# Attention and graph layers on one Trainium2 core: four-row tables, one ring of row tiles, deviations by logarithm, new step times

## Chip, core and metric

The kernel runs on one core of one Trainium2 chip. TensorE (PE in the profile) multiplies matrices into PSUM, VectorE (DVE) and ScalarE (ACT) work elementwise and along rows, GpSimd (POOL) makes small products and issues indirect DMAs, SyncE (SP) issues most other DMAs. Each engine runs its own instructions in program order and waits on semaphores for the others. The metric is device time in microseconds, as the median of several runs; the profile is one execution beside them.

## What is computed

```python
# x: (32, 512, 1024), adj: (512, 512), wq, wk: (512,), bm: (512,), bias: (1024,)
h = relu(layernorm(x))                       # over the last axis
q = einsum('c,bcn->bn', wq, h);  k = einsum('c,bcn->bn', wk, h)
s = leaky_relu(q[:, None, :] + k[:, :, None], 0.01)
agg = einsum('bcn,bmn->bcm', h, softmax(s, -1))
x = x + relu(einsum('oc,bcm->bom', adj, agg) + bm[None, :, None])
h = relu(layernorm(x))
x = x + einsum('bnf,nm->bmf', h, adj * adj) + bias
```

Everything is float32. The scores matrix has rank one before the leaky slope, so the kernel never forms it. It sorts the 1024 columns of a batch by q: for a given k the terms with positive score are a suffix of the sorted list, the others a prefix, and the weighted sums of all suffixes and prefixes give every output row.

## The kernel before

A batch passes through a chain of steps. `load` brings four row tiles of 128 x 1024, `stats`, `norm`, `slopes` and `relu` normalise them (lines 409 to 436: variance, square root on ScalarE, reciprocal on VectorE, then one activation a tile). `scores` gives q and k, `row` broadcasts q to all partitions through DRAM, `columns` turns q and k. `rank` (VectorE) counts for each column how many q are smaller, `lower` (ScalarE) how many are below -k. `value` multiplies h by adj's transpose, eight tiles of 128 columns, and `spread` copies each out of PSUM. `to_rows` turns ranks into table rows, `scatter` writes each value row (512 values and its q, 513 in all) into one of five DRAM tables at its sorted place. `fetch` reads the sorted table back in nine blocks, `weights` makes exponentials of q, and nine `scan` steps multiply a masked, weighted matrix with a block; each step does a suffix block and a prefix block in the two halves of TensorE's columns. `sums` copies each step's last row into the next block (the carry) and writes all sums to the table. `gather` fetches for each output column one suffix sum, one prefix sum and the single value between them as 3 x 513 values in one row; `excess`, `divide`, `weigh` and `combine` mix them, `turn` transposes the result and adds it to rows of x that `reload` has brought again. The second layer follows: `stats`, `norm`, `slopes`, `relu` into new h tiles, `lift` (bias), `propagate` (512 x 512 squares of adj) and `finish`, which adds and writes out.

What sets the order: every step has a time in the table `PLAN` for each of its parts, plus 80.647 for each batch; `FIRST` and `LAST` shift and stretch the times of the first and last five batches. All steps of all batches are sorted by these times and issued in that order, each engine getting its instructions in it. The numbers are only an order: the real distance between batches is what the engines make of it. In the middle of the run steps of four or five batches alternate, for instance values of batch 15 with scans of 13 and 14, propagates of 11 and turns of 12.

Row tiles come from three pools: `xp` with 7, `yp` with 7 and `hp` with 4 buffers; x tiles are loaded into `xp` (the second batch's and three of the third's into `yp`), reloaded y tiles into `yp`, h of layer 1 into `hp`. A tile's buffer is free after its last reader. Table i of the five holds slots of three rows (suffix sum, prefix sum, even value), and a second half for the odd values; 126 values and two fixed rows make one block of 128. The two fixed rows come from `pads`, one step with 20 DMAs on SP. `fetch` needs two DMAs per three blocks, for even and odd rows.

Of the kernel before, what the change touches and what calls it, by code (L numbers as in the profile page):

```python
# [10 lines left out]
BF16 = mybir.dt.bfloat16  # L11
# [9 lines left out]
DATA = 126  # L21
PAIRS = 63
# [3 lines left out]
TABLES = 5  # L26
PLAN = {
    "adjacency": (-108.2,),
    "biases": (103.637,),
    "columns": (-0.644,),  # L30
    "combine": (
        295.175, 296.981, 297.681, 298.56, 293.456, 294.898, 296.312, 299.441, 298.758,
        299.991, 297.356, 298.478, 299.289, 299.451, 296.18, 297.782,
    ),
    "compare_mask": (-39.924,),
    "divide": (279.776,),
    "excess": (274.084,),
    "factors": (31.052,),
    "fetch": (71.51,),
    "finish": (356.071, 361.635, 372.571, 377.123, 391.802, 417.732, 398.837, 420.531),  # L40
    "from_rows": (87.236,),
    "gather": (260.35, 264.453, 263.071, 264.447, 267.501, 263.458, 263.983, 262.344),
    "later": (82.669,),
    "lift": (343.707, 352.288, 361.264, 350.629),
    "load0": (-132.547,),
    "load1": (-83.561,),
    "load2": (-110.642,),
    "load3": (-58.45,),
    "lower": (25.135, 20.956, 15.44, 19.087, 14.733, 13.756, 46.166, 37.237),
    "masks": (-18.987,),  # L50
    "norm0": (-31.509,),
    "norm1": (326.35,),
    "pads": (-73.925,),
    "propagate": (346.423, 349.207, 352.169, 365.765, 371.233, 382.761, 381.981, 389.706),
    "rank": (17.984, 18.872, 20.129, 19.992, 25.594, 25.16, 26.367, 26.318),
    "reload0": (283.236,),
    "reload1": (289.947,),
    "reload2": (275.592,),
    "reload3": (294.126,),
    "relu0": (-21.389, -21.25, -20.652, -20.617),  # L60
    "relu1": (336.308, 336.463, 336.836, 338.53),
    "row": (1.149,),
    "scan": (88.672, 94.082, 102.974, 119.344, 135.342, 151.67, 171.394, 183.726, 197.836),
    "scatter": (49.236, 49.927, 49.759, 49.383, 53.226, 50.436, 50.301, 52.611),
    "scores": (-2.312,),
    "slopes0": (-23.106,),
    "slopes1": (327.104,),
    "spread": (10.418, 15.798, 4.081, 13.981, 26.765, 25.953, 18.654, 18.733),
    "square": (58.25,),
    "stationary": (82.87, 113.617, 158.362),  # L70
    "stats0": (-66.042, -57.278, -62.987, -37.25),
    "stats1": (317.836, 318.803, 321.449, 320.562),
    "sums": (90.354, 96.928, 115.433, 127.043, 139.894, 157.148, 175.982, 190.223, 211.407),
    "to_rows": (21.507, 28.041),
    "totals": (87.7,),
    "turn0": (305.575, 305.673, 305.631, 305.894),
    "turn1": (311.888, 311.406, 311.889, 311.693),
    "turn_adjacency": (-56.308,),
    "value": (4.654, 14.383, -2.141, 4.319, 19.868, 19.769, 15.801, 17.456),
    "weigh": (288.834, 288.645, 287.955, 288.582, 291.515, 291.657, 292.795, 290.433),  # L80
    "weights": (79.137,),
}
FIRST = {
    "columns": ((-42.337, 0), (-5.231, 0), (-2.394, 0), (1.4, 0), (-0.267, 0)),
    "combine": (
        (1.654, -0.5293), (1.005, -0.3379), (12.151, -0.5389), (4.662, 1.8664), (-2.717, -0.8902),
    ),
    "divide": ((-6.522, 0), (2.121, 0), (-5.673, 0), (4.125, 0), (-1.132, 0)),
    "excess": ((-1.018, 0), (2.997, 0), (-2.579, 0), (2.459, 0), (2.332, 0)),
    "factors": ((12.008, 0), (36.085, 0), (20.556, 0), (-17.001, 0), (38.59, 0)),  # L90
    "fetch": ((-13.827, 0), (-9.161, 0), (-4.562, 0), (-10.853, 0), (-1.955, 0)),
    "finish": (
        (-7.71, -0.5057), (2.749, -0.1853), (2.024, 0.1345), (-9.528, -0.7581), (-1.467, 0.1212),
    ),
    "from_rows": ((-16.545, 0), (143.901, 0), (-18.52, 0), (2.567, 0), (44.362, 0)),
    "gather": (
        (-9.577, -0.9485), (-11.32, -0.6577), (-4.449, 0.1722), (-9.629, -0.1251), (0.796, 0.0714),
    ),
    "later": ((-7.518, 0), (-7.347, 0), (-5.042, 0), (-3.972, 0), (4.883, 0)),
    "lift": (  # L100
        (18.493, -0.0414), (7.449, -0.8273), (15.021, 1.1896), (12.507, -0.3341), (13.391, 1.5716),
    ),
    "load0": ((-55.083, 0), (-28.454, 0), (-82.787, 0), (-89.755, 0), (-8.172, 0)),
    "load1": ((-101.05, 0), (-75.105, 0), (-63.613, 0), (-51.655, 0), (-0.85, 0)),
    "load2": ((-75.638, 0), (-49.315, 0), (-74.213, 0), (-72.717, 0), (-4.898, 0)),
    "load3": ((-124.613, 0), (-99.018, 0), (-53.784, 0), (-32.124, 0), (2.903, 0)),
    "lower": (
        (-42.973, -0.9302), (-15.708, -0.6946), (-9.312, -0.2971), (10.582, -0.0696), (34.856, -0.2988),
    ),
    "norm0": ((-83.601, 0), (-72.105, 0), (-7.68, 0), (-14.053, 0), (-0.379, 0)),  # L110
    "norm1": ((7.168, 0), (3.555, 0), (4, 0), (0.017, 0), (-5.5, 0)),
    "propagate": (
        (2.872, -0.6898), (4.018, -0.2375), (-1.06, -0.345), (-1.214, -0.2813), (-1.309, -0.0657),
    ),
    "rank": (
        (-28.589, 0.7379), (-2.87, -0.0721), (-9.055, 1.3394), (2.403, 0.1874), (-13.459, 0.0458),
    ),
    "reload0": ((-6.546, 0), (6.572, 0), (3.271, 0), (5.826, 0), (-6.189, 0)),
    "reload1": ((-1.43, 0), (8.813, 0), (6.594, 0), (3.913, 0), (-1.301, 0)),
    "reload2": ((-12.374, 0), (4.019, 0), (-0.514, 0), (8.006, 0), (-11.757, 0)),  # L120
    "reload3": ((1.756, 0), (10.208, 0), (8.663, 0), (2.721, 0), (1.743, 0)),
    "relu0": (
        (-45.821, -0.4234), (-30.012, 0.2683), (5.354, 1.299), (-1.745, 0.0153), (3.565, -0.5324),
    ),
    "relu1": (
        (9.188, 0.8499), (2.193, -0.013), (10.49, -0.8921), (-4.148, -0.0533), (5.006, -0.1977),
    ),
    "row": ((-24.758, 0), (-11.86, 0), (-11.402, 0), (-3.047, 0), (-12.236, 0)),
    "scan": (
        (-10.549, -0.0092), (-6.067, 0.0274), (-9.758, -0.1074), (-3.442, 0.0619), (-0.102, -0.002),  # L130
    ),
    "scatter": (
        (-17.315, 0.2618), (-11.153, 0.1679), (0.523, -0.1955), (-0.018, 0.156), (10.696, 0.3981),
    ),
    "scores": ((-62.327, 0), (-16.533, 0), (-8.214, 0), (-8.615, 0), (-9.042, 0)),
    "slopes0": ((-60.963, 0), (-35.582, 0), (0.527, 0), (-21.398, 0), (0.491, 0)),
    "slopes1": ((7.724, 0), (5.221, 0), (19.376, 0), (1.394, 0), (7.329, 0)),
    "spread": (
        (-20.028, 0.1376), (-6.015, 0.992), (8.718, 0.232), (10.947, -0.0528), (-1.297, 0.1468),
    ),  # L140
    "stationary": (
        (-9.533, -0.0517), (-0.489, 0.0893), (-5.756, -0.1735), (-6.449, -0.1248), (4.497, -0.0251),
    ),
    "stats0": (
        (-104.674, 0.702), (-77.356, 0.023), (-31.203, 0.8527), (-27.97, 0.4148), (-4.885, 0.5116),
    ),
    "stats1": (
        (1.142, 1.1308), (0.139, -0.1099), (5.326, 1.0258), (1.699, -0.7252), (-0.894, -0.2163),
    ),
    "sums": (  # L150
        (-8.312, -0.031), (-5.309, 0.0498), (-7.225, -0.0992), (-0.666, 0.0426), (1.428, -0.0107),
    ),
    "to_rows": (
        (-22.19, 0.5865), (-4.005, -0.1384), (-1.537, -0.1666), (6.658, -0.9288), (6.396, -0.6681),
    ),
    "totals": ((-8.637, 0), (-5.524, 0), (-8.905, 0), (-5.244, 0), (1.382, 0)),
    "turn0": ((-0.966, 0.9178), (2.05, 1.1944), (5.507, -0.2416), (13.541, 1.3559), (6.422, 0.711)),
    "turn1": (
        (-5.235, 2.5311), (3.046, 0.3048), (6.19, 0.6659), (-2.074, -0.6081), (-2.371, 1.8837),
    ),  # L160
    "value": (
        (-38.477, -0.2052), (-18.574, 0.6364), (-1.298, 0.5607), (-3.097, 0.6813), (-5.339, -0.0078),
    ),
    "weigh": (
        (-11.307, 0.6182), (-3.966, -0.0933), (3.637, 0.3643), (2.741, 0.6417), (-2.168, 0.2103),
    ),
    "weights": ((-7.839, 0), (-5.68, 0), (-3.274, 0), (-1.31, 0), (1.823, 0)),
}
LAST = {
    "columns": ((7.408, 0), (2.218, 0), (11.624, 0), (6.617, 0), (9.298, 0)),  # L170
    "combine": (
        (184.23, -0.647), (7.018, -0.6426), (4.54, 0.7582), (4.732, 1.7176), (6.572, -0.8403),
    ),
    "divide": ((175.719, 0), (2.439, 0), (-3.673, 0), (2.742, 0), (4.328, 0)),
    "excess": ((172.709, 0), (3.234, 0), (1.536, 0), (-5.245, 0), (8.713, 0)),
    "factors": ((-5.036, 0), (-12.606, 0), (17.188, 0), (-12.641, 0), (7.562, 0)),
    "fetch": ((5.667, 0), (1.995, 0), (5.156, 0), (-1.217, 0), (1.341, 0)),
    "finish": (
        (752.974, -0.831), (173.796, 0.1634), (35.432, 0.5906), (9.597, -0.1536), (9.066, 0.2434),
    ),  # L180
# [616 lines left out]
```

## Time and profile before

| | us |
|---|---|
| median of 3 runs | 2378.45 (2374.22 to 2379.13) |
| profiled execution, span | 2372.9 |
| TensorE busy | 2295.2 |
| VectorE busy | 1952.6 |
| ScalarE busy | 1599.8 |
| GpSimd busy | 720.7 |
| 123 table loads on ScalarE | 158 |

The span runs from the first to the last instruction of the profiled execution; it lies 5.55 us below the median of the runs. In the profile L703 is the matmul of propagate (pg), L550 of value (pv), L639 and L636 of a scan (sc), L696 of turn (tr), L445 of scores (pq). A float32 matmul appears as two records. The DMA engines moved 643 MB, a mean of 271 GB/s; in the middle of the run they are busy about 0.9 of the time.

### The profile page before, as it was taken

How to read it: one execution, taken by the hardware profiler on the slowest of the kernel's cores; microseconds unless marked ns; L12 is line 12 of the kernel's file. 1: busy time of each engine (PE TensorE's matmuls, PEld its weight loads, DVE VectorE, ACT ScalarE, POOL GpSimd, SP SyncE). 2: the span in 40 equal slices, each digit the busy share in tenths (PEclk: the TensorE clock that was granted, in tenths of full speed). 3: DMA queues.
4: the chain of work that ended last, by engine and by line, in shares of the span. 5: the costliest groups of instructions: out<-in, count | busy, mean ns of one | idle time of the engine just before them, and what ended most of it. 6: DMA issues, size and time to landing. Idle time of an engine off the chain costs nothing.

```text
span 2372.9 us, 28069 instructions
## 1 busy us (share of the span) xinstructions
PE 2295.2 (97%) x7568; PEld 1011.5 (43%) x7568; DVE 1952.6 (82%) x5008; ACT 1599.8 (67%) x2880; POOL 720.7 (30%) x973
## 2 busy tenths in 40 slices
PE   7787999999999999999999999999999999999997
PEld 3233444444444444444444444444444444443443
DVE  7457888888888888888888888888888888888875
ACT  4576776766777766777676777676677676677551
POOL 2233333233333233233223233323333323233310
PEclk9988999999999999999999999999999999999998
DMA  6678888989999998999999999899988898998972
GB/s 222 171 181 277 284 284 277 296 269 276 287 290 285 296 286 266 277 299 283 288 292 266 276 294 287 287 291 272 268 291 276 288 302 253 276 282 269 311 294 79
DMA packets 206894, 643.45 MB, mean 271 GB/s; under 512 B 29120, under 2 KB 29248, under 8 KB 206736
## 3 DMA queue, kind: packets, MB, share of 16 engines
q1 hardware_dynamic: 142944, 355.74, 53.9%
q0 software_dynamic: 57344, 268.99, 30.7%
q10 hardware_dynamic: 6448, 16.92, 2.3%
q8 instruction: 61, 1.00, 0.2%
q14 instruction: 97, 0.79, 0.1%
HBM read 429.94 MB, written 211.60 MB: 270 GB/s over the span
## 4 chain that ended last, share of the span: by engine, by line
PE 85%; DMA 5%; DVE 5%; ACT 2%; issue 1%; POOL 1%; SPq 0%; ACTq 0%; another core or an unknown queue 0%; POOLq 0%; DVEq 0%
PE pg L703 34%; PE pv L550 33%; PE sc L639 10%; PE tr L696 4%; DMA vs<-td 2%; PE pq L445 2%; PE sc L636 1%; DVE g L689 1%; DVE st L414 1%; DMA g<-td,idg 1%; DMA td<-v,idx 1%; DVE junk L492 1%; ACT x L433 0%; DVE junk L487 0%; DMA x<-in_x_dram 0%
## 5 line engine op out<-in xcount | busy, mean ns | idle before, releaser
L703 PE MATMUL pg<-h,wsq 128*128 128x512 f32 x2048 | 911.2, 598 | 12.8 <-ACT h L433 12.8
L550 PE MATMUL pv<-wmT,x 128*128 128x512 f32 x2048 | 908.8, 598 | 5.9 <-ACT x L433 4.4
L703 PEld LDWEIGHTS pg<-h,wsq 128*128 128x128 f32 x2048 | 382.8, 191 | 517.4 <-issue 476.1
L550 PEld LDWEIGHTS pv<-wmT,x 128*128 128x128 f32 x2048 | 382.0, 191 | 499.1 <-issue 452.6
L623 POOL TENSOR_TENSOR sm<-mask_a,wc 128x192 f32<-128x192 f32 x96 | 51.9, 540 | 1254.9 <-DVE wc L600 785.7
L689 DVE SCALAR_TENSOR_TENSOR g<-g,cf 128x512 f32<-128x512 f32 x512 | 357.9, 756 | 46.4 <-ACT g L685 44.3
L648 ACT COPY vs<-sc 1x512 f32<-1x512 f32 x256 | 145.3, 567 | 272.9 <-PE sc L639 208.6
L563 POOL DMA_INDIRECT td<-v,idx x256 | 272.4, 1064 | 149.3 <-POOL v L562 36.3
L639 PE MATMUL sc<-vs,sm 128*64 128x512 f32 x1024 | 282.6, 621 | 21.3 <-POOL sm L623 11.1
L503 ACT ACTIVATE junk<-qrow,qk 128x1024 bf16<-128x1024 f32 x256 | 294.0, 1148 | 5.5 <-DMA qrow<-qd 2.5
L660 POOL DMA_INDIRECT g<-td,idg x256 | 243.5, 951 | 147.4 <-issue 71.5
L698 DVE SCALAR_TENSOR_TENSOR y<-tr,nbm,y 128x512 f32<-128x512 f32 x256 | 174.4, 744 | 66.3 <-PE tr L696 61.2
L711 DVE SCALAR_TENSOR_TENSOR y<-pg,bm_sb,y 128x512 f32<-128x512 f32 x256 | 185.8, 731 | 32.4 <-PE pg L703 32.0
L651 ACT COPY t<-sc 128x512 f32<-128x512 f32 x288 | 168.0, 583 | 40.7 <-DMA td<-t 35.3
L433 ACT ACTIVATE x<-x,nmr,rstd 128x1024 f32<-128x1024 f32 x128 | 148.6, 1231 | 64.9 <-DVE nmr L425 64.9
L492 DVE TENSOR_SCALAR_CACHE_REDUCE junk<-qrow,qk,cnt 128x896 bf16<-128x896 f32 (+6 forms) x224 | 180.5, 806 | 8.2
L685 ACT ACTIVATE g<-g,cf 128x512 f32<-128x512 f32 x256 | 167.7, 712 | 6.4 <-DVE cf L679 5.3
L487 DVE TENSOR_SCALAR_CACHE_REDUCE junk<-qrow,qk 128x128 bf16<-128x128 f32 (+6 forms) x224 | 166.0, 741 | 6.6
L414 DVE BATCH_NORM_STATS2 st<-x 128x6 f32<-128x512 f32 x256 | 162.7, 677 | 9.6 <-DMA x<-in_x_dram 9.6
L439 DVE TENSOR_TENSOR y<-y,bias_sb 128x1024 f32<-128x1024 f32 x128 | 154.3, 1219 | 16.0 <-ACT h L433 16.0
L557 ACT COPY v<-pv 128x512 f32<-128x512 f32 x256 | 141.8, 579 | 29.7 <-PE pv L550 14.0
L414 DVE BATCH_NORM_STATS2 st<-y 128x6 f32<-128x512 f32 x256 | 160.4, 668 | 0.0
(111 smaller groups left out, 1923.1 us busy)
## 6 DMA issues: line engine op xcount, KB each, us to landing
vs<-td SPq DMA_DIRECT2D x192, 384.8 KB
td<-t SPq DMA_DIRECT2D x576, 128.2 KB
x<-in_x_dram SPq DMA_DIRECT2D x128, 512.0 KB
y<-in_x_dram SPq DMA_DIRECT2D x128, 512.0 KB
out_dram<-y SPq DMA_DIRECT2D x128, 512.0 KB
qrow<-qd ACTq DMA_DIRECT2D x32, 512.0 KB
td<-v,idx POOLq DMA_INDIRECT x256, 8.3
g<-td,idg POOLq DMA_INDIRECT x256, 13.8
```

What stands on the lines that cost most here:

```text
L414: nc.vector.bn_stats(st[:, i, :], s.x[c][:, ts(i, HALF)])
L492: nc.vector.tensor_scalar(junk[:, j * P :], s.qrow[:, j * P :], qc, first, ALU.is_lt, ALU.add, accum_out=s.cnt[:, 1, j : j + 1],)
L503: nc.scalar.activation(junk, s.qrow, AF.Sign, bias=s.qk[:, 1, j : j + 1], accum_out=s.sgn[:, j : j + 1])
L550: nc.tensor.matmul(pv, s.h[c][:, ts(j, P)], wmT[:, c, :], start=(c == 0), stop=(c == NC - 1))
L563: i = nc.gpsimd.indirect_dma_start(tds[s.b % TABLES][:, :], bass.IndirectOffsetOnAxis(ap=s.idx[j // 4][:, j % 4 : j % 4 + 1], axis=0), v[: ...
L639: nc.tensor.matmul(p[ts(k, HP), :], m[:, k, :], s.vs[h][:, 0:C], start=True, stop=True)
L651: nc.scalar.copy(t[:, 0:C], p)
L660: nc.gpsimd.indirect_dma_start(s.g[:, j, :], None, tds[s.b % TABLES][0 : 3 * NB * HP, :].rearrange("(s k) w -> s (k w)", k=3), bass.Indire ...
L689: nc.vector.scalar_tensor_tensor(r, s.g[:, j, k * W : k * W + C], s.cf[:, k, j : j + 1], r, ALU.mult, ALU.add)
L698: nc.vector.scalar_tensor_tensor(xh, pt, nbm[:, o : o + 1], xh, ALU.max, ALU.add)
L703: nc.tensor.matmul(pg, wsq[:, r, ts(c, P)], s.h[r][:, ts(i, HALF)], start=(r == 0), stop=(r == NC - 1),)
L711: nc.vector.scalar_tensor_tensor(xh, s.pg.pop((c, i)), bm_sb[:, c : c + 1], xh, ALU.add, ALU.add)
```

## The change

- The table has four rows per pair of ranks: suffix sum, even value, prefix sum, odd value. A block holds 124 values (`RUN` is 31 pairs, twice per block) and two pairs of fixed rows; even and odd ranks alternate over the partitions, so one DMA fetches three blocks. The gather still reads three neighbouring rows, which start at the suffix row; even value and prefix sum change places in them. The index formulas get shorter for `to_rows`.
- `pads` becomes five steps, one per table, with two DMAs each.
- All row tiles (x, y, h) come from one pool of 18 (`ROWS`).
- The deviation's inverse is exp(-0.5 ln(var + eps)) on ScalarE, both functions from one table set that is loaded at the start, and three small operations on VectorE refine it by a Newton step.
- `rank` and `lower` write their unused elementwise output as uint8, not bfloat16; the two masks are made directly; q is kept in four DRAM rows by turns, not two.
- `PLAN`, `FIRST` and `LAST` have new numbers, the last two for six batches; the distance of 80.647 stays.

```diff
-    NB = N // DATA + 1
+    NB = N // (4 * RUN) + 1
-    xp = ctx.enter_context(tc.tile_pool(name="xp", bufs=7))
-    yp = ctx.enter_context(tc.tile_pool(name="yp", bufs=7))
-    hp = ctx.enter_context(tc.tile_pool(name="hp", bufs=NC))
+    xp = ctx.enter_context(tc.tile_pool(name="xp", bufs=ROWS))
...
     def sorted_rows(td, h, n):
-        rows = td.rearrange("(o h s k) w -> o s h k w", o=2, s=HP, k=3)
-        return rows[:, :, h : h + n, 2, :]
+        rows = td.rearrange("(h p k) w -> p h k w", p=P, k=2)
+        return rows[:, h : h + n, 1, :]
...
-    nc.scalar.activation(root, eps_sb, AF.Sqrt)
+    nc.scalar.preload_act_table_set("natural_log_exp_and_others")
...
-    def pads(s):
-        pad = vp.tile([P, W], F32, tag="v", name="pad")
+    def pads(s, i):
+        pad = vp.tile([P, W], F32, tag="v", name=f"pad_{i}")
         nc.vector.memset(pad, 0.0)
         nc.vector.memset(pad[:, C : C + 1], FAR)
-        for td in tds:
-            for o in range(2):
-                nc.sync.dma_start(sorted_rows(td, 0, NB - 1)[o, 0], pad[0 : NB - 1, :])
-                nc.sync.dma_start(sorted_rows(td, NB - 1, 1)[o, :, 0], pad[0:HP, :])
+        halves = tds[i].rearrange("(g o k) w -> g o k w", o=HP, k=2)[0 : 2 * (NB - 1), 0:2, 1, :]
+        nc.sync.dma_start(halves, pad[0 : 2 * (NB - 1), :].unsqueeze(1).broadcast_to([2 * (NB - 1), 2, W]))
+        nc.sync.dma_start(sorted_rows(tds[i], NB - 1, 1)[:, 0], pad)
...
     def masks(s):
+        for mask, k in ((mask_a, 1), (mask_b, -1)):
+            nc.vector.memset(mask, 1.0)
+            nc.gpsimd.affine_select(
+                out=mask, in_=mask, compare_op=ALU.is_gt, fill=0.0, base=0, pattern=[[-2 * k, HP]],
+                channel_multiplier=k,
+            )
...
     def norm(s, layer):
-        nc.scalar.activation(s.std, s.mv[:, :, 1], AF.Sqrt, bias=eps_sb)
+        nc.scalar.activation(s.std, s.mv[:, :, 1], AF.Ln, bias=eps_sb)
+        s.rstd = sp.tile([P, NC], F32, tag=f"rstd{layer}", name=f"rstd{layer}_{s.b}")
+        nc.scalar.activation(s.rstd, s.std, AF.Exp, scale=-0.5)
     def slopes(s, layer):
-        nc.vector.reciprocal(s.rstd, s.std)
+        nc.vector.scalar_tensor_tensor(t, s.mv[:, :, 1], EPS, s.rstd, ALU.add, ALU.mult)
+        nc.vector.scalar_tensor_tensor(t, t, -0.5, s.rstd, ALU.mult, ALU.mult)
+        nc.vector.scalar_tensor_tensor(s.rstd, t, 1.5, s.rstd, ALU.add, ALU.mult)
...
     def relu(s, layer, c):
-            pool, tag = (xp, "x") if s.b == B - 2 else (hp, "h")
-            h = pool.tile([P, N], F32, tag=tag, name=f"h_{s.b}_{c}")
+            h = xp.tile([P, N], F32, tag="x", name=f"h_{s.b}_{c}")
...
     def rank(s, j):
-        junk = wp.tile([P, N], BF16, tag="junk", name=f"junk_{s.b}_{j}")
+        junk = wp.tile([P, N], U8, tag="junk", name=f"junk_{s.b}_{j}")
...
+    def floor(rk, n, name, s):
+        f = sp.tile([P, rk.shape[1]], F32, tag=f"floor{name}", name=f"floor{name}_{s.b}")
+        nc.vector.tensor_scalar(f, rk, 1.0 / n, 0.5 / n - 0.5, ALU.mult, ALU.add)
+        nc.vector.tensor_scalar(f, f, ROUND, -ROUND, ALU.add, ALU.add)
+        return f
     def to_rows(s, i):
-        pair, block = pairs(rk, "q", s)
-        odd = 3.0 * NB * HP
-        nc.vector.tensor_scalar(rk, rk, odd, 5.0, ALU.mult, ALU.add)
-        nc.vector.scalar_tensor_tensor(rk, pair, 3.0 - 2.0 * odd, rk, ALU.mult, ALU.add)
+        f = floor(rk, 2 * RUN, "q", s)
+        nc.vector.tensor_scalar(rk, rk, 2.0, 5.0, ALU.mult, ALU.add)
-        nc.vector.scalar_tensor_tensor(s.idx[i], block, 3.0, rk, ALU.mult, ALU.add)
+        nc.vector.scalar_tensor_tensor(s.idx[i], f, 4.0, rk, ALU.mult, ALU.add)
     def from_rows(s):
-        pair, block = pairs(rk, "r", s)
+        pair = floor(rk, 2, "p", s)
+        f = floor(pair, RUN, "r", s)
-        nc.vector.scalar_tensor_tensor(s.idg, pair, 1.0, block, ALU.add, ALU.add)
+        nc.vector.tensor_tensor(f, f, pair, ALU.add)
+        nc.vector.tensor_scalar(s.idg, f, 4.0, 4.0, ALU.mult, ALU.add)
...
     def fetch(s):
-            for o in range(2):
-                d = nc.sync.dma_start(t[ts(o, HP)], sorted_rows(tds[s.b % TABLES], 3 * i, 3)[o])
+            d = nc.sync.dma_start(t, sorted_rows(tds[s.b % TABLES], 3 * i, 3))
...
     def sums(s, i):
-        td = tds[s.b % TABLES].rearrange("(s k) w -> s k w", k=3)
+        td = tds[s.b % TABLES].rearrange("(s k) w -> s k w", k=4)
         nc.sync.dma_start(td[ts(ha, HP), 0, :], t[0:HP, :])
-        nc.sync.dma_start(td[ts(hb, HP), 1, :], t[HP:P, :])
+        nc.sync.dma_start(td[ts(hb, HP), 2, :], t[HP:P, :])
```

Of the new times, those that the prediction speaks of, as they stand for the batches in the middle of the run:

```diff
-    "adjacency": (-108.2,),
+    "adjacency": (-988.26,),
-    "fetch": (71.51,),
+    "fetch": (33.445,),
-    "scan": (88.672, 94.082, 102.974, 119.344, 135.342, 151.67, 171.394, 183.726, 197.836),
+    "scan": (51.176, 57.633, 64.219, 81.673, 97.074, 108.292, 133.694, 146.062, 161.601),
-    "turn0": (305.575, 305.673, 305.631, 305.894),
+    "turn0": (264.575, 264.492, 264.401, 264.843),
-    "value": (4.654, 14.383, -2.141, 4.319, 19.868, 19.769, 15.801, 17.456),
+    "value": (-34.236, -39.683, -34.816, -23.667, -14.904, -27.47, -22.782, -17.741),
```

## The prediction

> **What bounds the kernel now.** I read the page first (busy shares and slices), then the chain that ended last, then TensorE's timeline at the head, in one steady batch and at the end.
>
> ```profile
> PE 2295.2 (97%) x7568; PEld 1011.5 (43%) x7568; DVE 1952.6 (82%) x5008; ACT 1599.8 (67%) x2880; POOL 720.7 (30%) x973
> ...
> PE   7787999999999999999999999999999999999997
> ...
> PEclk9988999999999999999999999999999999999998
> ```
>
> TensorE is busy 97% of the span; what it misses lies in the first four slices and the last. The chain puts a number on the middle:
>
> ```profile
> 440.35 3.63 PE pv L550 x8
> ...
> 510.88 3.63 PE pv L550 x8
> ```
>
> The same step of consecutive batches starts 70.53 us apart, and the stage between has TensorE 100% busy at full clock. 32 x 70.53 = 2257; the span is 2372.9. So 116 us are head and tail, and a change pays only there, or by shortening the 70.53. VectorE has about 61 us of work per batch, ScalarE 50: neither is the bound. In one batch (the chain again):
>
> ```profile
> 1086.36 3.28 PE sc L639 x12
> 1089.64 17.36 PE pv L550 x40
> 1107.00 1.87 PE sc L639 x8
> ...
> 1128.30 0.86 PE sc L636 x2
> ...
> 1142.95 1.01 PE sc L639 x4
> ```
>
> A scan step is 0.86 us in the full array (L636). In 64-column halves (L639, 4 records a step) one step takes 1.01 and two 1.87, so entering that mode costs 0.15; the 40 pv after it take 17.36 instead of 40 x 0.429 = 17.17, so leaving costs 0.19. Three steps should take 2.73 and take 3.28: 0.55 us is a stall, because two of them are consecutive steps of one batch and the second needs the row that ScalarE carries over.
>
> The head, TensorE's timeline (last bracket: idle before, and its releaser):
>
> ```profile
> 118.58 2.43 PE L639 MATMUL sc<-vs,sm 128*64 128x512 f32 x4 [4.39 <-POOL sm L623]
> ...
> 206.56 2.08 PE L636 MATMUL sc<-vs,sm 128*128 128x512 f32 x2 [8.93 <-ACT vs L649]
> ...
> 214.15 4.91 PE L696 MATMUL tr<-ident,g 128*128 128x128 f32 x32
> ...
> 263.34 17.43 PE L703 MATMUL pg<-h,wsq 128*128 128x512 f32 x40
> ```
>
> TensorE waits for scans whose rows were scattered and fetched late, then for the first gather.
>
> **What the Trainium skill says.** TensorEngine Tiling (Array Packing), Key Properties: changing the tiling mode drains TensorE; the 0.15 + 0.19 us above agree. TensorE: Matmul & The Clock Gate, What's actually happening: after an idle window of about 3.4 us the array runs at half clock; the trace agrees (32 transposes after the stalls took 4.91 us, in the steady batches 3.5). ScalarE: Activation LUTs, What ACT_TABLE_LOAD costs and Table sets: each load about 1283 ns, and one set holds both exp and ln; the trace has 1283 ns on each of 123 loads, and no run yet shows the joint set. DMA: Bandwidth & Descriptors, Why a DMA increments its semaphore by 16: 64 and 128 partitions both divide by 16 engines, so a merged fetch is no faster per byte; this trace cannot say.
>
> **The change, part by part.** *Deviations.* 61+28+27+6+1 table loads go: 123 x 1.283 = 158 us of ScalarE; one preload stays. Sqrt becomes Ln (as 0.298) plus an Exp (as B's exp, 0.209): +64 x 0.209 = 13 us. VectorE loses 64 reciprocals (11 us) and gains 3 x 64 small operations at 0.163 = 31 us: +20. ScalarE falls to about 1455 us. In the steady stage TensorE's 70.53 hides all of it; without that cover ScalarE's gain would be 4.5 us a batch.
>
> *Four-row tables.* to_rows drops 3 of 8 operations at 0.17 twice a batch (-34 us VectorE), from_rows gains one (+5); with the above, VectorE nets -9 us. Fetch goes from six DMAs to three (4.06 us of SP issue for six, so 2 us less per batch), same bytes; gather and write-back move the same bytes in the same row lengths. Row stride 4 instead of 3 and uint8 junk: nothing in the trace prices either; no reason for a gain, a loss bounded by DMA's free tenth (0.92 share) and VectorE's slack. I take 0.
>
> *Pads* go from one step of 20 DMAs to five of 2 (about the same bytes), spread behind other loads; *square*, masks and adjacency move to the very front. Adjacency is 1 MB ahead of batch 0's rows: at the 283 GB/s of the first 20 us, +3.7 us. One pad memset and the mask memsets (behind wsq's 3.6 us on POOL) now stand between batch 0's statistics and its slopes on VectorE: +2.5. adjacency's transposes (2.3 us) leave the time after scores. A new wait: table 3's pad takes one of the eight v tiles after all eight hold batch 0's values, so its memset on VectorE waits for the first scatter (about 52 us by the walk below); behind it stand statistics of batch 2 and rank of batch 1, which wait for the row broadcast until 60 anyway: 0, or up to 8 us at that point if scatter starts late. First pv: 20.4 + 3.7 + 2.5 + 0.6 (Ln/Exp, three more operations) - 2.3, less about 1 of masks that fill waiting = about 23.6 us.
>
> *Row ring.* 7+7+4 tiles become 18 shared. By the plan's times the shortest gap from last use to next load in the steady stage is 10.8 plan units (before: 2.3); no wait costed. SP holds loads behind fetches as before.
>
> *New times*, the part that decides. I sorted the steps by the new plan numbers and walked the head with this trace's durations: value or propagate 3.43, scan 0.9, scores 1.9, one batch's turn 3.5, rank 2.0 each on VectorE, scatter 1.45 a call on POOL, 3 to 8 us to land, fetch 10 to 11, row broadcast 10 to 11 from scores, a scan's carry 1.85 on ScalarE, gather 8 x 1.24 + 16, sixteen combines 11. "Work ahead" is TensorE work at full rate earlier in program order; time minus it is what was lost.
>
> - First pv: before 20.4 - 3.9 = 16.5 lost; after 23.6 - 3.7 = 19.9.
> - First scan of batch 1: before 118.6 - 79.9 = 38.7. After: scores of batch 1 now precede value 0's last tile, so seven value steps hide batch 0's fetch. But ScalarE's queue holds lower(1), weights(0), sums(0) and relu(2) one after another, and scores(2) start at 97; fetch(1) is issued at 99.5, lands at 110, weights 115, scan at 117 to 118: 38.8. No gain.
> - First scan of batch 2: before 171.1 - 117.4 = 53.7. After: value 2 ends at 144, scatter to 148, landed 155, fetched 167, scan about 171: 54.
> - turn of batch 0: before 214.2 - 142.7 = 71.5. Gather 0 stands behind batch 2's stationary on POOL, as before: 170 to 180, landed 196, divide and combine to about 207: 208.5 - 141.8 = 67.
> - First propagate: before 263.3 - 182.4 = 80.9; there it lost 4.1 us to batch 3's fetch. After, scan 3 stands three values later and its rows land at 222, needed at 230: 250 - 181.5 = 68.5. **Head: -12.4 us.**
>
> *Steady batch.* New order: scans 0 and 6, two values, scan 1, two values, scans 2 and 7, value, three pg, scans 8 and 3, three pg, scan 4, pg, turn, pg, turn, scan 5, scores. No two consecutive steps of one batch touch: -0.55. One more entry into and exit from 64-column mode: +0.34. Net -0.21 x about 24 batches = **-5.0**.
>
> *Tail.* The last turn, statistics, slopes, relu and 64 pg keep their order; that chain gets the Exp and three small operations for one: +0.6. relu now goes rows 2, 0, 3, 1 while pg reads 0, 1, 2, 3, so row 1 comes fourth with three pairs (0.86 each) behind it: +1.7. Four pg of batch 29 instead of three cover relu(30), where TensorE waited 1.8: -1.8. **Tail +0.5.**
>
> ```profile
> 2337.72 30.41 PE L703 MATMUL pg<-h,wsq 128*128 128x512 f32 x64 [10.29 <-ACT h L433]
> ```
>
> Sum: 2372.9 - 12.4 - 5.0 + 0.5 = 2356.0 for a profiled execution. The median of the runs stood 5.55 us over this profile; carried over, **2361.5**.
>
> **Rivals.** *A, the head packs tighter (0.18).* My walk adds one landing time after another at loaded values. If scatters land in 3 us and fetches in 8, batches 1 and 2 start 5 to 9 us earlier each, and gather 0 follows. For it: ScalarE is relieved exactly there (a load stands on the head's chain at 93.6 us). Against: the gaps are mostly DMA. Head loss 45: 2361.5 - 23.5 = 2338.
>
> *B, VectorE becomes late for the turn in every batch (0.17), the slow side.* From the den copy (waits for TensorE at 48 us of the batch) VectorE runs without a pause through from_rows, rank, statistics, lift, combine: 46.6 us by the durations above, and the last combine that turn 0 needs is done 2.4 us before TensorE gets there; five combines of the other half are mixed in ahead or behind. The slack in plan units between combine and turn 0 falls from 6.1 to 3.2. For it: VectorE already waited 44 us in all for weigh. Against: that run was 49 us before and TensorE waited at it only in the tail (0.9 us). From 2.4 us on every microsecond costs 25 (batches); from 3.3 it is slower than before; at 3.6: 2361.5 + 30 = 2391.
>
> *C, no change (0.13).* Head gains are lost where the first full batches overlap (gather 1 waits for the single gather tile, scan 4), or the uint8 or table writes eat the 0.21: 2378. That tables still load between Ln and Exp (the preloaded set not kept) belongs here: 64 x 2 x 1.283 on ScalarE is hidden in the middle, 5 to 8 us in the head.
>
> **How the numbers follow.** Mine 0.52, its own range 2350 to 2373; A 0.18, B 0.17, C 0.13. 0.2% (4.8 us) is about what a measurement tells from no change. Faster: 0.49 of mine and all of A, 0.67; same: 0.03 and 0.12 of C, 0.15; slower: B and a rest, 0.18. The range goes from A's 2340 to most of B, 2388.
>
> **What would show it.** Right: one table load; ScalarE near 1455 us; steady start-to-start near 70.3, with no x12 scan; first propagate near 250, first pv near 23.6; final idle near 11. Wrong: a DVE releaser before tr in the middle (B); propagate at 230 (A) or 262 (C); DMA share at its ceiling.

## The result and the profile after

The changed kernel takes 2365.37 us (median of 5 runs, 2361.12 to 2368.44), the kernel before, on the same chip, 2378.45 (5 runs, 2373.27 to 2380.82). The ratio is 0.9948, 95% interval 0.9933 to 0.9963: faster by 0.5%. The prediction was 2361.5, with 2340 to 2388 as its range. The profiled execution spans 2363.6 us (before 2372.9; predicted 2356.0).

The page after, busy shares and the slices of TensorE and its clock:

```profile
PE 2290.4 (97%) x7568; PEld 1006.6 (43%) x7568; DVE 1954.1 (83%) x4981; ACT 1441.9 (61%) x2821; POOL 734.0 (31%) x971
...
PE   7898999999999999999999999999999999999997
...
PEclk8998999999999999999999999999999999999998
```

ScalarE lost 158 us of work; the prediction had 145, 158 of table loads less 13 of Exp. VectorE is where it was (predicted 9 us less). One table load is left, where there were 123:

```profile
L510 ACT ACT_TABLE_LOAD x1 | 1.3, 1283 | 0.8 <-PEq L957 0.8
```

TensorE is still the bound, with its gaps at the two ends. The chain of the changed kernel over one batch in the middle, beginning and ending with the same step of two consecutive batches:

```profile
1069.48 3.63 PE pv L724 x8
...
1080.54 1.76 PE sc L812 x8
1082.31 7.07 PE pv L724 x16
1089.37 1.01 PE sc L812 x4
1090.38 7.07 PE pv L724 x16
1097.45 1.87 PE sc L812 x8
1099.31 3.63 PE pv L724 x8
...
1139.70 3.63 PE pv L724 x8
```

The distance is 70.22 us, where before it was 70.53, and there is no group of three steps (x12) any more. TensorE's timeline of the changed kernel in the head, just behind it, and at the end (last bracket: idle before, and its releaser):

```profile
24.11 5.08 PE L724 MATMUL pv<-wmT,x 128*128 128x512 f32 x8
...
197.33 0.33 PE L869 MATMUL tr<-ident,g 128*128 128x128 f32 x1 [2.37 <-DVE g L862]
...
226.43 0.28 PE L785 MATMUL pd<-w,mask_a 128*64 128x9 f32 x2 [2.68 <-ACT w L762]
...
250.46 7.13 PE L876 MATMUL pg<-h,wsq 128*128 128x512 f32 x16
...
351.12 3.96 PE L869 MATMUL tr<-ident,g 128*128 128x128 f32 x19 [3.97 <-DVE g L862]
375.36 1.11 PE L812 MATMUL sc<-vs,sm 128*64 128x512 f32 x3 [1.79 <-POOL sm L796]
500.07 0.65 PE L869 MATMUL tr<-ident,g 128*128 128x128 f32 x4 [0.88 <-DVE g L862]
638.24 1.86 PE L869 MATMUL tr<-ident,g 128*128 128x128 f32 x15 [0.49 <-DVE g L862]
...
2328.18 2.08 PE L876 MATMUL pg<-h,wsq 128*128 128x512 f32 x2 [12.58 <-ACT h L613]
```

The first propagate starts 12.9 us earlier than before (263.34). Then something is new: four waits in batches that had none before, three of them for the last combine of VectorE ahead of a turn. To see what that costs I cut each execution at three places: the first propagate, the `pr` matmuls (columns) of the thirteenth batch, which I call batch 12, and those of batch 24. All times are starts in TensorE's timeline, the last column goes to the end of the last matmul. The experiments below are in the table already.

| kernel | first propagate | to batch 12 | period, 12 to 24 | batch 24 to end |
|---|---|---|---|---|
| before | 263.3 | 533.3 | 70.53 | 725.2 |
| after | 250.5 | 541.6 | 70.22 | 724.5 |
| before + Ln and Exp | 263.6 | 535.4 | 70.53 | 724.7 |
| before + ring | 261.3 | 538.9 | 70.53 | 730.4 |
| before + scan order | 265.8 | 538.5 | 70.22 | 728.8 |
| before + tables | 249.3 | 533.2 | 70.53 | 724.7 |
| before + tables, six fetches | 261.4 | 535.5 | 70.56 | 737.9 |
| all parts, times of before | 245.8 | 532.9 | 70.53 | 721.7 |
| after, Sqrt again | 244.9 | 551.2 | 70.22 | 728.6 |
| after, batch 2 mixed earlier | 242.9 | 547.8 | 70.22 | 726.0 |
| after, last relu sorted | 240.2 | 539.4 | 70.22 | 725.2 |
| after, x rows first | 235.0 | 540.6 | 70.22 | 725.2 |

From before to after: -12.9, then +8.3, then -3.7 (12 x 0.305), then -0.6: together -8.9 of the 9.3 us between the two spans. About 0.9 us of the first two is no gain and no loss: in the new order one scan step (four records, 118 before and 114 after) stands behind the first propagate and not ahead of it. That leaves 12.0 us gained in the head and 7.4 given back within ten batches, more than half. The 7.1 us of the four waits are nearly all of it.

One execution is not a measure of the head: the kernel with the last relu sorted is the changed kernel up to its last batch, and it starts the first propagate at 240.2 and not 250.5. What repeats is this. With six transfers for each fetch the first propagate starts at 261.3 to 265.8 us; with the merged fetch, whatever the order, at 235.0 to 250.5. Between the first propagate and batch 12 TensorE is idle for 5.5 to 12.4 us in all five kernels with the new times, and for 0.1 to 3.8 us in the nine with the old ones.

### The profile page after: what moved, and what is told of

Read it like the earlier page. It is cut to its first block, busy times and chain, and to the rows that moved or that the text cites. A ratio compares the mean times of both kernels' runs of the same rounds, so it can differ in the third digit from the quotient of the medians.

```text
span 2363.6 us, 27844 instructions
## 1 busy us (share of the span) xinstructions
PE 2290.4 (97%) x7568; PEld 1006.6 (43%) x7568; DVE 1954.1 (83%) x4981; ACT 1441.9 (61%) x2821; POOL 734.0 (31%) x971
## 4 chain that ended last, share of the span: by engine, by line
PE 78%; DVE 8%; DMA 7%; ACT 3%; POOL 1%; issue 1%; SPq 0%; ACTq 0%; DVEq 0%; POOLq 0%
PE pg L876 31%; PE pv L724 31%; PE sc L812 8%; PE tr L869 4%; PE pq L625 2%; DMA vs<-td 2%; DVE st L591 2%; DMA g<-td,idg 1%; DVE g L862 1%; ACT junk L683 1%; DMA td<-t 1%; PE sc L809 1%; DMA td<-v,idx 1%; DVE junk L672 1%; ACT h L613 1%
## 5 line engine op out<-in xcount | busy, mean ns | idle before, releaser
L724 PE MATMUL pv<-wmT,x 128*128 128x512 f32 x2048 | 920.8, 601 | 0.7 <-DVE step L602 0.7
L737 POOL DMA_INDIRECT td<-v,idx x256 | 281.5, 1100 | 247.2 <-POOL v L736 46.4
L683 ACT ACTIVATE junk<-qrow,qk 128x1024 uint8<-128x1024 f32 x256 | 294.0, 1149 | 11.5 <-DMA qrow<-qd 9.6
L812 PE MATMUL sc<-vs,sm 128*64 128x512 f32 x1024 | 268.9, 616 | 10.2 <-ACT vs L821 5.6
L672 DVE TENSOR_SCALAR_CACHE_REDUCE junk<-qrow,qk,cnt 128x512 uint8<-128x512 f32 (+6 forms) x224 | 180.5, 806 | 8.2
L667 DVE TENSOR_SCALAR_CACHE_REDUCE junk<-qrow,qk 128x512 uint8<-128x512 f32 (+6 forms) x224 | 165.4, 738 | 21.7 <-DMA qrow<-qd 16.7
L613 ACT ACTIVATE h<-y,nmr,rstd 128x1024 f32<-128x1024 f32 x128 | 151.7, 1234 | 17.9 <-DMA out_dram<-y 8.3
```

Of the source, the lines that this page charges most:

```text
L613: nc.scalar.activation(h, s.x[c], AF.Relu, bias=s.nmr[:, c : c + 1], scale=s.rstd[:, c : c + 1])
L672: nc.vector.tensor_scalar(junk[:, j * P :], s.qrow[:, j * P :], qc, first, ALU.is_lt, ALU.add, accum_out=s.cnt[:, 1, j : j + 1],)
L683: nc.scalar.activation(junk, s.qrow, AF.Sign, bias=s.qk[:, 1, j : j + 1], accum_out=s.sgn[:, j : j + 1])
L724: nc.tensor.matmul(pv, s.h[c][:, ts(j, P)], wmT[:, c, :], start=(c == 0), stop=(c == NC - 1))
L737: i = nc.gpsimd.indirect_dma_start(tds[s.b % TABLES][:, :], bass.IndirectOffsetOnAxis(ap=s.idx[j // 4][:, j % 4 : j % 4 + 1], axis=0), v[: ...
L812: nc.tensor.matmul(p[ts(k, HP), :], m[:, k, :], s.vs[h][:, 0:C], start=True, stop=True)
```

## Experiments

Each ratio is taken against the kernel before on the same chip; the chips differ by up to 13 us in that kernel's median, so times from different chips are not subtracted.

**One part of the change at a time, on the kernel before.** First the deviations:

```diff
-    nc.scalar.activation(root, eps_sb, AF.Sqrt)
+    nc.scalar.preload_act_table_set("natural_log_exp_and_others")
...
-        nc.scalar.activation(s.std, s.mv[:, :, 1], AF.Sqrt, bias=eps_sb)
+        nc.scalar.activation(s.std, s.mv[:, :, 1], AF.Ln, bias=eps_sb)
...
+        nc.scalar.activation(s.rstd, s.std, AF.Exp, scale=-0.5)
```

(and the three operations of the Newton step for the reciprocal).

> The kernel before with one edit: the deviations by Ln and Exp from one table set instead of Sqrt and a VectorE reciprocal. My theory: ScalarE is not the bound in the steady batches, so its relief is worth nothing there; the steady period stays at 70.53 us and the whole run changes by -3 to +1 us. Rival (ScalarE's relief is where the gain is): about 160 us less ScalarE work moves the end by -10 us or more, with a shorter steady period.

Measured: ratio 1.0010 (1.0002 to 1.0018), so 0.5 to 4 us slower, at or just past the slow end of my theory, and the period stays at 70.53. ScalarE went from 1599.8 to 1453.1 us busy and the run got no faster. The rival is out.

The ring:

```diff
-    xp = ctx.enter_context(tc.tile_pool(name="xp", bufs=7))
-    yp = ctx.enter_context(tc.tile_pool(name="yp", bufs=7))
-    hp = ctx.enter_context(tc.tile_pool(name="hp", bufs=NC))
+    xp = ctx.enter_context(tc.tile_pool(name="xp", bufs=18))
```

(and `load`, `reload` and `relu` take their tiles from it).

> The kernel before with one edit: one ring of 18 row tiles for x, y and h in place of rings of 7, 7 and 4. My theory: no matmul of before waits for a row tile, so 0 us (within 2). Rival (the ring holds work back at the head or the tail): -3 us or more, seen in an earlier first propagate.

Measured: 0.9990 (0.9982 to 0.9999), about -2 us, with an interval from 0 to -4 that takes in the rival's -3; the first propagate was at 261.3 (263.3). Small, as expected. Its row in the table is of the longest of its 14 executions, 8.6 us above their median.

The tables, with fetch, masks and index formulas; the pads stay one step, at its old time:

```diff
-            for o in range(2):
-                d = nc.sync.dma_start(t[ts(o, HP)], sorted_rows(tds[s.b % TABLES], 3 * i, 3)[o])
+            d = nc.sync.dma_start(t, sorted_rows(tds[s.b % TABLES], 3 * i, 3))
...
         for td in tds:
-            for o in range(2):
-                nc.sync.dma_start(sorted_rows(td, 0, NB - 1)[o, 0], pad[0 : NB - 1, :])
-                nc.sync.dma_start(sorted_rows(td, NB - 1, 1)[o, :, 0], pad[0:HP, :])
+            halves = td.rearrange("(g o k) w -> g o k w", o=HP, k=2)[0 : 2 * (NB - 1), 0:2, 1, :]
+            nc.sync.dma_start(halves, pad[0 : 2 * (NB - 1), :].unsqueeze(1).broadcast_to([2 * (NB - 1), 2, W]))
+            nc.sync.dma_start(sorted_rows(td, NB - 1, 1)[:, 0], pad)
```

> The kernel before with the four-row tables, the single fetch and the new masks and pads, all other steps at their old times. My theory: fewer transfers of the same rows, all hidden in the steady batches: 0 to -3 us, from the head alone, and the steady period stays at 70.53. Rival (the shorter chain from the sums to the gathers is what lets the head pack tighter by itself): first propagate earlier by 5 us or more without any new times, and -5 us or more at the end.

Measured: 0.9933 (0.9918 to 0.9948), 16 us. My theory of 0 to -3 is out and the rival right in what it expected: without one new time the first propagate comes 14 us earlier (263.34 before), and the table above shows that nothing of it is given back.

```profile
249.32 17.43 PE L693 MATMUL pg<-h,wsq 128*128 128x512 f32 x40
```

The rival put the gain between the sums and the gathers; the two kernels part earlier, at the first fetch. SP's and ScalarE's timelines of the kernel before, and then of the one with the new tables (SPq and ACTq are DMA issues):

```profile
52.82 4.06 SPq L580 DMA_DIRECT2D vs<-td  x6
60.19 0.51 ACTq L451 DMA_DIRECT2D qd<-qr  x1
67.07 0.34 ACTq L456 DMA_DIRECT2D qrow<-qd  x1
67.45 0.19 ACT L587 COPY w<-zero 128x2 f32<-128x2 f32 x1 [6.07 <-DMA qd<-qr]
```

```profile
52.80 1.44 SPq L570 DMA_DIRECT2D vs<-td  x3
60.20 0.51 ACTq L448 DMA_DIRECT2D qd<-qr  x1
63.18 0.34 ACTq L453 DMA_DIRECT2D qrow<-qd  x1
63.90 0.20 ACT L577 COPY w<-zero 128x2 f32<-128x2 f32 x1 [2.51 <-DMA qd<-qr]
```

Both issue the fetch at 52.8 and the small write of q (4 KB) at 60.2. Behind three transfers the write is back 3.9 us earlier than behind six, and ScalarE, which waits for it ahead of `weights`, starts the chain of scans 3.6 us sooner. The write is issued on ScalarE's queue and the fetch on SP's, yet behind the longer fetch the write lands later. Other parts of the tables differ too, so the next run takes the fetch alone.

**Is it the fetch?** The same kernel with six transfers again:

```diff
-            d = nc.sync.dma_start(t, sorted_rows(tds[s.b % TABLES], 3 * i, 3))
+            for o in range(2):
+                d = nc.sync.dma_start(t[ts(o, HP)], sorted_rows(tds[s.b % TABLES], 3 * i, 3)[ts(o, HP)])
```

> The kernel before with the four-row tables as in the run of the tables alone (0.9933 of before), but each fetch issued as six transfers of 64 rows again in place of three of 128. My theory after that run: the merged fetch carries the gain, because each fetch of the head stands on the chain and its last transfer is issued 2.3 us earlier, and the row of scores queued behind it is back 3.8 us earlier. So the gain falls from 16 us to 0 to 6 (ratio 0.9975 to 1.000). Rival (fewer VectorE steps and the shorter pads carry it): the gain stays at 11 to 16 us (ratio 0.993 to 0.9955).

Measured: 1.0049 (1.0034 to 1.0063), 12 us slower than before, so the merged fetch is worth some 27 us in these tables, and not 10 to 16. A piece of this kernel's chain in the head and its first propagate; then the queue that SP's transfers use (packets, MB, share of 16 engines), with six transfers and with three:

```profile
59.94 7.17 DMA qd<-qr
```

```profile
261.44 17.43 PE L694 MATMUL pg<-h,wsq 128*128 128x512 f32 x40
```

```profile
q1 hardware_dynamic: 142944, 355.91, 55.7%
```

```profile
q1 hardware_dynamic: 141408, 355.90, 52.7%
```

The q write takes 7.17 us again and the first propagate is back at 261.4; that part is as my theory had it. The difference builds up from batch to batch: the first scan of batch 1 starts at 118.6 us before, at 110.0 with the tables and at 117.5 with six transfers in them; that of batch 2 at 171.1, 162.6 and 171.9; the first turn at 214.2, 202.7 and 212.6. A second part was in no theory: the stretch from batch 24 to the end is 13 us longer than with three transfers, with one wait of 9.4 us for the weights there. For the same bytes the packets of SP's queue (q1) hold 55.7% of 16 engines' time instead of 52.7%. Why six transfers cost more in these tables than in the old ones I have not settled. The Trainium skill, DMA: Bandwidth & Descriptors, Rules for kernel authors, says that two transfers to disjoint partition halves serialize and that one of 128 partitions should be used in their place; these runs agree that one transfer is better and show what it is worth here; that the halves serialize is not seen in these traces. My prediction had looked only at the bytes: it took from the page that 64 and 128 partitions spread over the same 16 engines, and from that, which the page does not say, that merging gains nothing per byte.

**The order of the scans alone.**

```diff
             t = s.b * T + t + shift + stretch * (t - mean)
+            if name in ("scan", "sums") and n == 1 and 5 <= s.b < B - 5:
+                t += 3.8
```

> The kernel before with one edit: scan step 1 and sums step 1 of batches 5 to 25 stand 3.8 plan units later, so that no two scan steps of one batch follow each other on TensorE. My theory: the stall of 0.55 us between them goes, one more group of 64-column matmuls costs 0.34 us, so the steady period falls from 70.53 to about 70.3 us and the run by 4 to 7 us. Rival (the entry into the 64-column mode is all that counts): the period rises by 0.3 us and the run is 5 to 8 us slower.

Measured: 0.9986 (0.9976 to 0.9995), 1 to 6 us faster, where my theory had 4 to 7, and the period is 70.22, exactly the one of the changed kernel. Its chain has the pattern of the changed kernel too (x8, x4, x8 in place of x12, x8):

```profile
1092.75 1.76 PE sc L639 x8
1094.51 7.06 PE pv L550 x16
1101.58 1.01 PE sc L639 x4
```

This one edit is the whole gain of the steady batches. In the profiled execution, 8 us above this kernel's median, TensorE also waited 3.8 us in all for VectorE between the first propagate and batch 12, so waits for VectorE in early batches are not the new times' alone.

**Parts of the changed kernel undone or mended.** Sqrt and reciprocal back, all new times kept (the first diff of this section, reversed):

> The changed kernel with the deviations taken back to Sqrt and reciprocal (table loads and VectorE reciprocals return), all new times kept. My theory: +2 to +5 us against the changed kernel (about 2367 to 2370 us), lost at the head and the tail where the deviations stand on the chain; the steady period stays at 70.22. Rival (ScalarE's relief carries the gain): +10 us or more, and a steady period back at 70.5.

Measured: 1.0030 (1.0021 to 1.0038), slower than before by 7 us. On the same chip the changed kernel with only the order of its last relu mended (below) had 0.9937, some 21 us less. Neither theory: the period stays 70.22, so it is not the steady batches, but my +2 to +5 is far off. Between the two profiles the loss is 4.7 us in the head, 11.8 from the first propagate to batch 12 and 3.4 at the end. TensorE's waits of this kernel and then of the changed one (us in total, times, longest):

```profile
PE tr L866 <- DVE g L859: 11.9, 7, 2.4
...
PE pg L873 <- DVE y L881: 5.4, 1, 5.4
```

```profile
PE tr L869 <- DVE g L862: 9.5, 5, 4.0
```

The longest of these is new: 5.4 us ahead of a propagate, for VectorE to finish a y tile. Under the old times Sqrt cost nothing against Ln and Exp (Ln and Exp had 1.0010 above). Why it costs so much under the new ones is open. VectorE does not have too much work there: from 250 to 540 us it is busy for 237 us with Sqrt, 243 in the changed kernel and 253 in the kernel before. So what makes it late is not the sum of its work but its order, or what it waits for in that order.

The longest wait of the changed kernel, 3.97 us, stands at the turn of batch 2, so I moved that batch's mixing ahead (three entries of the table, put on one line here):

```diff
 FIRST["divide"][2], ["weigh"][2], ["combine"][2]: shift
-    -4.843, -1.738, 3.109
+    -14.5, -12.5, -17.0
```

> The changed kernel with divide, weigh and combine of batch 2 moved ahead (starts -14.5, -12.5 and -17.0), so that combine of batch 2 stands on VectorE before the lifts and finishing of batch 1. My theory: the wait of 3.97 us at the turn of batch 2 is VectorE being late because of that order, so it goes, and the run is 3 to 4 us faster than the changed kernel (about 2361.5 us). Rival (the gathers set the time, and the wait only moves on): 0 us, with a wait of the same size at a later turn or propagate.

Measured: 0.9975 (0.9965 to 0.9985), about 9 us slower than the changed kernel with the mended relu on the same chip. TensorE waits at 270.7, 343.9, 360.3, 369.9, 498.3 and 636.9 us, 0.9 to 2.4 each and 9.9 in sum, four of them for VectorE: the stretch to batch 12 is 547.8. My theory is out. But the edit was aimed at a wait that belonged to one execution: the two kernels below have the same order there, and at the turn of batch 2 they wait 1.05 and 0.40 us in place of 3.97. What goes with it in VectorE's timeline is the gather. In the changed kernel the first operation that mixes batch 2 waits for it:

```profile
320.39 0.17 DVE L842 TENSOR_TENSOR cf<-g,arg 128x8 f32<-128x8 f32 x1 [4.18 <-DMA g<-td,idg]
```

It waits 4.18 us here, 1.18 in the second of these executions and not for the gather in the third. So a gather that lands late can make VectorE late, as the rival had it; but that is three executions, and no experiment moved the gather alone.

The last relu in the order in which propagate reads it:

```diff
+        if name == "relu1" and s.b == B - 1:
+            times = tuple(sorted(times))
```

> The changed kernel with the last batch's first relu in the order of its tiles 0, 1, 2, 3 in place of 2, 0, 3, 1. My theory: the wait ahead of the last propagate falls from 12.6 to about 10.9 us and the run by 1.7 us (about 2363.7 us). Rival (the chain behind it, not this wait, sets the end): 0 us.

Measured: 0.9937 (0.9922 to 0.9953). Beside the changed kernel's 0.9948 that is within the intervals; in the trace the last wait is 11.45 in place of 12.58 us (12.58 and 12.57 in two more kernels with the old order). So the wrong order costs 1.1 us of wait, not 1.7, and the time cannot confirm even that.

The first batch's rows ahead of the adjacency (four entries, put on one line here):

```diff
-    "adjacency": (-988.26,), "square": (-559.865,), "masks": (-130.916,), "turn_adjacency": (-328.788,)
+    "adjacency": (-200.0,), "square": (-100.0,), "masks": (-123.0,), "turn_adjacency": (-106.0,)
```

> The changed kernel with the first batch's x rows loaded ahead of the adjacency and its squares, and the masks built behind the first slopes. My theory: the first value of batch 0 starts at about 20 us in place of 24, and up to 3.5 us of it carry to the end (about 2362 us). Rival (the chain of the first scans, gathers and VectorE steps sets the first propagate, so that TensorE only waits longer later): 0 us, with the first propagate still at 250 us.

Measured: 0.9929 (0.9912 to 0.9946). The first value starts at 20.1 and the first propagate at 235.0, against 24.1 and 240.2 in the run before on the same chip; the last matmul ends 4.0 us earlier. The four us at the first value are shown. That they carry to the end is not: the traces are on the side of my theory, but the first propagate moves by 10 us between two executions of one order, and the ratios cannot tell.

**The structure without the new times.** All parts of the change (tables, ring, Ln and Exp, uint8; q stays in two DRAM rows and the pads in one step) in the order of the kernel before, with the edits shown above:

> All structural parts of the change (four-row tables with merged fetch, one ring, Ln and Exp, comparisons into uint8) under the times of the kernel before. My theory of the prediction: the new times carry the head's gain, so this is only 3 to 5 us faster than before (ratio 0.998 to 0.9987). Rival, from the run of the tables alone: the tables carry it, so this gives 12 to 18 us (ratio 0.9925 to 0.995), at least as much as the whole change, with the steady period still 70.53 us; then the new times, which shorten the period by 0.3 us, give their gain back somewhere else.

Measured: 0.9922 (0.9907 to 0.9938), 18 us. The rival is right: the parts alone do at least as well as the whole change (12 us; the two intervals just overlap). TensorE's waits of this kernel for VectorE's combine:

```profile
PE tr L684 <- DVE g L677: 0.5, 1, 0.5
```

One, in the tail. The same operations in another order, and the waits of the early batches are gone: the stretch to batch 12 is 532.9 against 541.6. So the give-back comes with the new times, or with what else this kernel lacks of the change, the five steps of the pads and the four rows for q; no run separates these. Which of the new times, I have not found. Nor does the head need them: 245.8 here, 235.0 to 250.5 with them. The uint8 outputs have no run of their own.

**Putting the winners together.** Tables, ring and the scan edit, with Sqrt; then the same with Ln and uint8:

> The kernel before with the four-row tables, one ring and scan step 1 of batches 5 to 25 moved behind two values; Sqrt, the other times and the comparisons as before. My theory: the gains add, 16 us of the head and 0.3 us in each of some 20 batches, so 20 to 23 us (ratio 0.990 to 0.9915) and a steady period of 70.22 us; it beats both kernels. Rival: VectorE is late for the turn in batches 4 to 8 once the period is shorter, as in the run of the scans alone, and the sum is no more than the tables' (ratio 0.993 or above).

> All structural parts of the change under the times of the kernel before, as in the run of the parts (0.9922 of before), and scan step 1 and sums step 1 of batches 5 to 25 later by 3.8 plan units. My theory: the gain in the head (first propagate near 246 us) and the shorter period (70.22 us) add, because under the old times VectorE is never late for a turn before 2100 us even with ScalarE and VectorE on Ln and Exp; 23 to 26 us below before (ratio 0.989 to 0.9905), the fastest of all. Rival: with the shorter period VectorE, which carries some 27 us more than with Sqrt, is late for the turn in the early batches as under the new times, and the ratio stays at 0.992 or above, with several us of waits of the transposes for the combine.

Measured: 0.9913 (0.9897 to 0.9928) and 0.9922 (0.9907 to 0.9937). Both have the period 70.22, the first propagate at 245.0 and 244.6, and no wait of a turn for VectorE's combine before 2100 us. The first is as my theory had it and beats both kernels: its interval lies below the changed kernel's. The second has the shortest profiled span of all, 2341.7, in the fastest of its five runs; its ratio is where the rival put it, without the waits that the rival named, and does not show the step beyond the parts alone that I expected. It ran on a chip where the kernel before takes 2365.8. Whether Ln or Sqrt is better in this order is not decided.

## Why the prediction was right, and where it was not

The median was missed by 3.9 us. The sign of the whole was right, and so was the mechanism of the steady batches and, in part, of the tail; that the number came so close is in good part luck. Point by point:

- **Head, -12.4.** First propagate predicted at 250, measured 250.5. But the working behind it is not confirmed. I gave the head to the new times, and of the merged fetch ("so 2 us less per batch") nothing went into the sum. That is the step that failed. The steady batches hide those 2 us, the head does not: there the fetch, and the small write behind it, stand on the chain, and the tables with the merged fetch give 14 us with the old times. The points on the way do not fit my walk either. First value at 24.1 (23.6; the terms that I listed add up to 23.9) and scan of batch 1 at 118.1 (117 to 118) are as predicted, but scan of batch 2 is at 163.8 (171) and the turn at 197.3 (208.5). The seven us at batch 2 are 3.6 of a scatter that landed at 151.4 and not 155, 1.3 of a fetch that landed 10.7 us after it and not 12, and 2.3 between fetch and scan. I then expected 41.5 us from that turn to the first propagate, and it took 53: the rows of scan 3 landed at 226 and not 222, and TensorE ran at a granted clock of 0.89 from 200 to 250. Two errors cancelled, and in four more executions with the new times, each with another small edit, the first propagate was at 235.0 to 244.9: the 250.5 is luck.
- **Behind the head.** The sum carried the head's gain to the end. It lost 7.4 us up to batch 12, 7.1 of them in the four waits shown. Three of these are rival B, VectorE late for the turn, in a form I had not priced: not in all 25 batches, only in early ones, and at 0.5 to 4 us each. Why only there is open; VectorE has no more work there than before the change. The slack between combine and turn that I read off (6.1 down to 3.2 plan units) was the right sign; I applied it to the steady batches alone, where it held.
- **Steady, -0.21 a batch.** Measured -0.305. The direction and both terms were right; the mis-sized one is the stall, by this estimate. The first scans of the batch follow the small `pd` matmuls, which are in the 64-column mode already: 1.76 for two steps there against 1.87 elsewhere, so this group pays no 0.15 to enter. Three steps should then take 2.6 us, not 2.73, and the stall in the 3.28 was about 0.66. With 0.34 for the extra entry and exit that gives -0.32.
- **Tail, +0.5.** Batch 24 to end: -0.6. The last wait grew by 2.3 us, as the two terms of my sum had it (10.29 to 12.58; the "final idle near 11" among my signs does not fit that sum), and the 1.8 us ahead of propagate 30 went. Of the two terms the 0.6 for the deviation came as predicted: 10.91 in the run of the parts, which has the old order. The order of the relu is worth 1.1 and not 1.7, and 0.5 are not accounted for. The rest of the 0.6 lies in other waits of the tail.
- **Profile to median, +5.55.** Measured +1.8 for the changed kernel. In every run on record the time is 1.6 to 1.8 us above the span of the same execution; the rest of the 5.55 is that the profiled execution of the kernel before was shorter than its median. 3.8 us of the 7.6 that the profile stood above my 2356.0 were hidden by it.
- **VectorE -9, ScalarE 1455.** VectorE: +1.5. Ln and Exp alone cost it 25 us (20 predicted), the tables alone saved 28 (29); the other 5 are not traced. ScalarE: 1453.1 with Ln and Exp alone, 1441.9 in the whole change. Neither is the bound, and the time does not show these errors.
- **Rivals.** A (head packs tighter): with the rows first the propagate came to 235, not 230, and the end gained only part of it. C (no change) is out as a number, and so are its table loads; but its first reason, that gains of the head are lost where the first full batches overlap, is what happened to more than half of them, mostly at VectorE's combine and not at the places it named.

## What to carry to other kernels

A saving that the steady state hides can still be worth more than the rest of the change in the head, where transfers stand one behind the other: cost it once per stage, not once per kernel. Here two half-partition transfers into one tile were worth merging, and a small write on another queue came back 3.9 us sooner for it. When a change brings parts and a new order together, run the parts in the old order before believing the new one, and check each engine's slack in the first batches after the head, not only in the steady ones. And take no single wait of one execution for a property of the kernel before a second execution shows it.

## What the hardware showed that was not expected

- The head is not one number. The changed kernel and the one with the sorted last relu are the same program up to the last batch, yet the first propagate was at 250.5 in one execution and 240.2 in the other, on another chip. TensorE was idle 40.6 and 36.9 us of the first 250, and the mean granted clock there was 0.92 and 0.95. The Trainium skill, TensorE: Matmul & The Clock Gate, What's actually happening, gives a reason, that an idle window of about 3.4 us brings the half clock. The eight first value records, behind a wait of 8.9 us and one of 1.2, took 5.08 us in the first execution and 3.74 in the other, where the same waits stand ahead of them; so the waits alone do not settle it. Of the 10.2 us between the two executions only 3.7 are idle time; the rest is in matmuls that took longer. So a few us between two single profiles of the head mean nothing without the ratio.
- A group of 64-column matmuls behind other 64-column matmuls shows no cost of entry: 1.76 us on the chain for two scan steps, 1.87 for two behind full-width ones.
- One table set does serve exp and ln: 1 table load of 1283 ns in place of 123.
